# A graph network layer: the turning of h moved from TensorE to DMA, ahead of its use

## The chip, the cores and the metric

The kernel runs on one core of a Trainium2 chip. The metric is device time in microseconds (us) of one launch. PE is TensorE (PEld its weight loads), DVE is VectorE, ACT is ScalarE, POOL is GpSimd, SP is SyncE, which here only issues DMAs.

## What is computed

64 graphs of 256 nodes with 256 channels, float32. After a layer norm without weights and a ReLU, `h` goes through one network layer:

```python
h = jnp.maximum(_layernorm(x, axis=-1), 0.0)
x = x + _L0_gnn_ref(h, adj, ...)
# inside, with x = h:
xc = jnp.transpose(x, (0, 2, 1))
h = relu(_bn(_conv1d(xc, conv1_w, 0), bn1...))        # 1 tap
h = _bn(_conv1d(h, conv2_w, 8), bn2...)               # 17 taps
x_conv = jnp.transpose(relu(h + xc), (0, 2, 1))
s = x @ w_se.T + b_se
A = jnp.exp(-dist(s)) * mask                          # mask is adj
msg = relu(x @ w_msg.T + b_msg)
x_nmp = jnp.einsum('bnm,bmd->bnd', A, msg)
gi = concat([x_conv, x_nmp]) @ w_ih.T + b_ih
gh = x @ w_hh.T + b_hh
r, z = sigmoid(gi_r + gh_r), sigmoid(gi_z + gh_z)
return (1 - z) * tanh(gi_n + r * gh_n) + z * x
```

## The kernel before, in words

**Tiling.** A block `i` is two graphs (W = 512 nodes); there are 32 blocks. Four blocks make a batch `b` of eight graphs; the eight batches run one after the other. In the loop `i = 4b` is the batch's first block and `nxt = i + 4` the first of the next batch, so that block numbers such as `nxt + 2` mean work done ahead.

**From x to hT.** `load_x` brings a block of rows to `x` (two buffers), with nodes on partitions. `norm_steps` (L507) makes the statistics on DVE (L518 to L523), the power -0.5 on POOL (L524) and scales `x` in place on DVE (L527). `transpose_h` (L590) turns the block on PE: eight 128x128 transposes against the identity (helper at L484) into `aux` banks of PSUM, and two ReLUs on ACT (L600) write `hT`, with channels on partitions. Then it issues the load of block `i + 2`. `hT` feeds `conv1`, `message`, `gates` and `residual`.

**The convolution of 17 taps** is done for a batch at a time in a transformed domain. `conv1` (w_c1 on PE, ReLU on ACT to `h`) and `split_steps` (DVE, writes U and V) prepare each block of the next batch; `forward` puts the odd and even forward transforms (DVE) in the planner's queue; `products` (eight calls a batch) multiplies by weights `wb`, streamed from DRAM by SP with nine buffers; `branch_back`, `q_back`, `p_back` and `join` go back on DVE, and `residual` (L719, then ReLU L720 on ACT) leaves x_conv in `Yv`. V and Yu are one memory.

**The rest of a block.** `message` makes msg and s; `embed` and `affinity` make exp(-dist) (L760, L761) and multiply by `ADJ` on DVE (L767); `aggregate` makes `xnm`; `gates` (L794) is called twice a block, once for each half of the output channels, and does 36 matmul passes of 128x512: the terms of h and xnm first, those of `Yv` last, with a hook `early` after the first third and `wait` ahead of the terms of `Yv`. `finish` turns the result back on PE (8 transposes), adds it to `Y` and stores it.

**adj.** Its columns are wanted in the order of `Yv`. From block 3 on `turn_adj` turns a block by a DMA transpose (512 KB, as pairs of uint16 halves) into the tile `halves` (one buffer), `keep_adj` writes it to DRAM in four DMAs of 1 KB rows (L403), `load_adj` (POOL queue) brings it back, and `join_adj` puts the halves together in two copies on ACT (L423). Before the change it is called at the end of `aggregate`.

**What sets the order.** Each engine runs its instructions in the order of the program, which is written out by hand. DVE work without a fixed place goes through `pace` (L234): a queue of steps that are put between the fixed DVE instructions where a running estimate of PE's and DVE's time leaves room; `pace.flush(mark)` empties it up to a mark. SP and POOL issue their DMAs in order too, and an issue that waits holds all behind it.

Of the kernel before, what the change touches and what calls it, by code (L numbers as in the profile page):

```python
# [301 lines left out]
def kernel(  # L302
# [122 lines left out]
    def load_y(i):  # L425
        Y[i] = late.tile([P, G * MC, D], FP, name="y", bufs=2)
        load_rows(Y[i], x, i, nc.gpsimd)
# [78 lines left out]

    def norm_steps(i):  # L507
# [5 lines left out]
        def stats(j):  # L513
            if j == 0:
                t["st"] = work.tile([P, G * MC, 6], FP, name="st")
                t["mv"] = work.tile([P, G * MC, 2], FP, name="mv")
                t["rstd"] = work.tile([P, G * MC], FP, name="rstd")
            nc.vector.bn_stats(t["st"][:, j, :], X[i][:, j, :])  # L518

        def aggregate_stats():  # L520
# [3 lines left out]
            nc.gpsimd.tensor_tensor(t["rstd"], t["rstd"], neg_half, ALU.pow)  # L524

# [63 lines left out]
    def transpose_h(i):  # L589
# [11 lines left out]
        if i + 2 < B // G:  # L601
            load_x(i + 2, nc.gpsimd if i < 2 else nc.sync)

# [178 lines left out]
    def aggregate(i):  # L782
# [8 lines left out]
        join_adj(i + 1)  # L791
# [49 lines left out]
    def finish(i):  # L841
# [8 lines left out]
        if i + 2 < B // G:  # L850
            load_y(i + 2)
# [11 lines left out]
    odd, even, normed, halved = (Mark() for _ in range(4))  # L863
# [53 lines left out]
    for b in range(NB):  # L917
# [17 lines left out]
        pace.flush(even)  # L935
        pace.add(fft.branch_back(Yv, T, 2))
        pace.add(fft.odd_back(Yv, T))
        aggregate(i)
        if b == 0:
# [6 lines left out]
        norm(nxt)  # L946
        affinity(i + 1)
        if b > 0:
            load_adj(i + 2)
        products(b, 6)  # L950
        if b == 0:
            transpose_a(i + 1)
        transpose_h(nxt)
        products(b, 7)
        pace.add(mix(fft.p_back(Yu, T), fft.q_factors(Yu)))
# [4 lines left out]
        stats, scale = norm_steps(nxt + 1)  # L960
        join(0)
        pace.add(stats)
        join(1)
        pace.add(scale, normed)
        pace.add(split_steps(nxt), halved)
        join(2)
        join(3)
# [109 lines left out]
```

## Time and profile before

| | |
|---|---|
| median of 12 runs (lowest to highest) | 1891.92 us (1886.38 to 1898.74) |
| the profiled execution's own time | 1889.53 us |
| its span, first to last instruction | 1887.5 us |
| mean granted clock of TensorE | 0.993 |
| DMA moved | 217.63 MB, mean 115 GB/s |
| `message(i + 2)` of batch 2 starts at | 617.38 us |
| `message(i + 2)` of batch 3 starts at | 839.01 us |

The first batch's inputs and the weights' transforms fill the first 120 us or so; a batch in the middle takes 839.01 - 617.38 = 221.6 us. Such a batch has a stage of `products` (about 57 us), in which SP streams `wb`, and a long stage of `gates` (about 165 us), in which the next batch is prepared. A row of a timeline gives start, duration, engine, line, operation, output and inputs, count, and in brackets the idle time of the engine before it with what ended it. A PE row's duration runs over into the next, so durations are taken here from start to start.

### The profile page before, as it was taken

What the parts mean: (1) busy time and instruction counts of PE and PEld (TensorE: products, weight loads), DVE (VectorE), ACT (ScalarE), POOL (GpSimd) and SP (SyncE); (2) the same over time, 40 slices, a digit from 0 to 9 for tenths busy, and PEclk for the clock granted to TensorE, in tenths of its full rate; (3) what the DMA queues carried; (4) which work ended last, traced back from release to release, by engine and by line L of the source; (5) the groups of instructions that cost most, each with busy time, mean ns of one, the idle gap of its engine ahead of it and who ended that gap; (6) DMA issues with size and microseconds to landing.
All of it is one profiled execution on the core that took longest, in us unless ns stands there. A gap on an engine that the chain in (4) does not pass through costs nothing.

```text
span 1887.5 us, 21985 instructions
## 1 busy us (share of the span) xinstructions
PE 1831.2 (97%) x7710; PEld 1137.2 (60%) x7710; DVE 1398.0 (74%) x2675; ACT 637.4 (34%) x1335; POOL 215.3 (11%) x340
## 2 busy tenths in 40 slices
PE   6999999999999999999999999999999999999997
PEld 3686454865459554784458655495546944587443
DVE  5878548996499946998389964999459983798522
ACT  2524332254222532244222443134432352224321
POOL 3210111010111010111101101110101111010000
PEclk9999999999999999999999999999999999999999
DMA  6886431761328341482316623284314823063010
GB/s 186 266 277 154 89 79 45 214 160 56 81 62 246 88 107 38 133 220 63 82 41 198 170 58 86 47 243 108 91 55 109 243 56 78 23 183 108 1 45 23
DMA packets 178526, 217.63 MB, mean 115 GB/s; under 512 B 85378, under 2 KB 105118, under 8 KB 178417
## 3 DMA queue, kind: packets, MB, share of 16 engines
q1 hardware_dynamic: 144373, 153.87, 28.9%
q0 software_dynamic: 31936, 60.48, 12.9%
q10 hardware_dynamic: 2108, 1.89, 0.3%
q8 instruction: 61, 1.00, 0.2%
q14 instruction: 48, 0.39, 0.1%
HBM read 156.54 MB, written 44.30 MB: 106 GB/s over the span
## 4 chain that ended last, share of the span: by engine, by line
PE 82%; DVE 8%; DMA 3%; issue 3%; ACT 2%; POOL 1%; POOLq 0%; ACTq 0%; DVEq 0%
PE acc L480 70%; PE aux L480 8%; PE aux L484 3%; DVE Yv L59 1%; PE aux L760 1%; DVE e L767 1%; DVE Yv L62 1%; DMA points<-points 1%; DVE T L65 1%; DVE Yv L65 1%; DMA x<-in_x_dram 1%; DMA wb<-filt 1%; POOL filt L648 1%; DVE msg L732 1%; DVE V L65 1%
## 5 line engine op out<-in xcount | busy, mean ns | idle before, releaser
L480 PE MATMUL acc<-hT,w_hh 128*128 128x512 f32 x768 | 354.6, 598 | 3.6 <-ACT h L619 3.6
L480 PE MATMUL acc<-xnm,w_ih 128*128 128x512 f32 x768 | 353.7, 595 | 0.0
L480 PE MATMUL acc<-Yv,w_ih 128*128 128x512 f32 x768 | 341.1, 593 | 9.6 <-ACT Yv L720 9.6
L480 PEld LDWEIGHTS acc<-Yv,w_ih 128*128 128x128 f32 x768 | 145.2, 190 | 196.5 <-issue 177.3
L480 PEld LDWEIGHTS acc<-xnm,w_ih 128*128 128x128 f32 x768 | 145.8, 191 | 183.6 <-issue 181.6
L480 PEld LDWEIGHTS acc<-hT,w_hh 128*128 128x128 f32 x768 | 143.8, 192 | 171.6 <-issue 161.9
L821 ACT ACTIVATE tr<-acc,b_rz 128x512 f32<-128x512 f32 x64 | 44.0, 687 | 542.0 <-PE acc L480 542.0
L823 DVE SCALAR_TENSOR_TENSOR gn<-tr,gn 128x512 f32<-128x512 f32 x64 | 44.2, 691 | 210.2 <-ACT tr L821 210.2
L849 POOL DMA_DIRECT2D out_dram<-y x64 | 39.0, 615 | 890.7 <-DVE y L848 860.9
L480 PE MATMUL acc<-U,wb 128*128 128x128 f32 x1024 | 124.8, 276 | 1.0 <-DMA wb<-filt 1.0
L480 PE MATMUL acc<-V,wb 128*128 128x128 f32 x1024 | 124.8, 275 | 0.0
L480 PEld LDWEIGHTS acc<-U,wb 128*128 128x128 f32 x1024 | 120.5, 192 | 4.9 <-DVE Yv L59 2.3
L59 DVE SCALAR_TENSOR_TENSOR V<-T,V 128x256 f32<-128x256 f32 (+2 forms) x224 | 121.6, 612 | 0.3
L480 PE MATMUL acc<-hT,w_c 128*128 128x512 f32 x256 | 117.8, 604 | 1.9 <-ACT hT L600 1.0
L480 PEld LDWEIGHTS acc<-V,wb 128*128 128x128 f32 x1024 | 119.5, 192 | 0.0
L480 PE MATMUL aux<-e,msg 128*128 128x256 f32 x464 | 104.9, 379 | 0.0
L480 PEld LDWEIGHTS aux<-e,msg 128*128 128x128 f32 x464 | 86.1, 190 | 11.4 <-issue 1.0
L848 DVE TENSOR_TENSOR y<-aux,y 128x512 f32<-128x512 f32 x64 | 41.1, 684 | 68.4 <-PE aux L484 68.4
L524 POOL TENSOR_TENSOR rstd<-rstd,neg_half 128x4 f32<-128x4 f32 x32 | 36.3, 1134 | 470.9 <-DVE rstd L523 470.8
L480 PE MATMUL aux<-w_msg,hT 128*128 128x259 f32 x384 | 89.4, 382 | 0.0
L527 DVE TENSOR_SCALAR x<-x,mv,rstd 128x256 f32<-128x256 f32 x128 | 44.3, 409 | 52.1 <-POOL rstd L524 52.1
L480 PEld LDWEIGHTS acc<-hT,w_c 128*128 128x128 f32 x256 | 49.2, 194 | 51.9 <-issue 45.6
(149 smaller groups left out, 2741.8 us busy)
## 6 DMA issues: line engine op xcount, KB each, us to landing
wb<-filt SPq DMA_DIRECT2D x376, 256.0 KB
y<-in_x_dram POOLq DMA_DIRECT2D x64, 256.0 KB, 5.4
out_dram<-y POOLq DMA_DIRECT2D x64, 256.0 KB, 5.2
x<-in_x_dram SPq DMA_DIRECT2D x60, 256.0 KB
halves_d<-halves SPq DMA_DIRECT2D x116, 128.0 KB
adjh<-halves_d POOLq DMA_DIRECT2D x116, 128.0 KB, 5.3
filt<-fo POOLq DMA_DIRECT2D x20, 252.0 KB, 5.4
filt<-fo SPq DMA_DIRECT2D x16, 252.0 KB
```

Source lines behind the costliest of these rows:

```text
L59: return self.step(out, lambda: self.v.scalar_tensor_tensor(out, x, s, y, op0=ALU.mult, op1=ALU.add))
L62: return self.step(out, lambda: self.v.tensor_add(out, x, y))
L65: return self.step(out, lambda: self.v.tensor_sub(out, x, y))
L480: nc.tensor.matmul(p, w, v, **kw)
L484: nc.tensor.transpose(p, v, ident)
L524: nc.gpsimd.tensor_tensor(t["rstd"], t["rstd"], neg_half, ALU.pow)
L527: nc.vector.tensor_scalar(X[i][:, j, :], X[i][:, j, :], t["mv"][:, j, 0:1], t["rstd"][:, j:j + 1], ALU.subtract, ALU.mult)
L648: eng.dma_start(out=filt[m][g * KG:g * KG + size].rearrange("k t c o -> (k t) (c o)"), in_=t[:size * kinds])
L821: nc.scalar.activation(tr, pr, AF.Tanh, bias=b_rz[:, dc:dc + 1], scale=0.5)
L823: nc.vector.scalar_tensor_tensor(gn, tr, 1.0, gn, op0=ALU.add, op1=ALU.mult)
L848: nc.vector.tensor_add(row_tile(Y[i], g), p, row_tile(Y[i], g))
L849: nc.gpsimd.dma_start(out=rows(out, G * i + g), in_=row_tile(Y[i], g))
```

## The change

The first five blocks still go the old way. From block 5 on (blocks 5 to 31, 27 in all) h is made thus:

- No scaling of `x` on DVE. Two small operations (DVE, POOL) make `shift` beside `rstd`.
- `turn_h`: four activations on ACT write relu(x * rstd + shift) into the tile `hh`, in blocks of 64 channels; a DMA transpose on SP (`hh` to `halves`, 512 KB from SBUF to SBUF); then the load of `x`.
- `sort_h`: four DMAs on SP in rows of 1 KB bring `halves` to a second `hh` (the same buffer).
- `join_h`: two copies on ACT put the halves together in `hT`.

`halves` has one buffer, shared by the turnings of h and of adj, and `hh` one, shared by the source of the turning and the sorted rows. The calls stand one ahead of the other: in a batch `turn_h(nxt + 1)` stands behind `message(i + 2)`, `join_h(nxt + 1)` in the second `gates`, `turn_h(nxt + 2)` right behind it, and so on; `turn_h(nxt + 4)` stands in the fifth `gates` and is joined in the next batch's `products`, where that block is `nxt`.

Moved are: `conv1(nxt)` from ahead of the first `gates` into its `wait`; `embed` and `affinity` into the hooks of `gates`; `conv1(nxt + 1)` ahead of `aggregate(i + 2)`; `join_adj` out of `aggregate`; the statistics of `nxt + 1` into `products`; `forward` ahead of `gates(i + 2, 0)`; the last two `join`s later. `Y` has one buffer in place of two.

What this does to the order on three engines is shown in the third batch (b = 2). **PE**, from the end of the first `gates` on (`Yv,w_ih` are the last terms of a call of `gates`, `ident,x` is a turning of h, `e,msg` is `aggregate`, `w_c` is `conv1`). Before:

```order
L480 MATMUL acc<-Yv,w_ih 128x512 x6
L480 MATMUL acc<-hT,w_hh 128x512 x4
L480 MATMUL acc<-xnm,w_ih 128x512 x4
L480 MATMUL acc<-hT,w_hh 128x512 x2
L480 MATMUL acc<-xnm,w_ih 128x512 x2
L480 MATMUL acc<-Yv,w_ih 128x512 x6
L484 MATMUL aux<-ident,x 128x128 x8
L480 MATMUL aux<-e,msg 128x256 x8
L480 MATMUL acc<-hT,w_c_95 128x512 x4
```

and now:

```order
L480 MATMUL acc<-hT,w_c_95 128x512 x4
L480 MATMUL acc<-Yv,w_ih 128x512 x6
L480 MATMUL acc<-hT,w_hh 128x512 x4
L480 MATMUL acc<-xnm,w_ih 128x512 x4
L480 MATMUL acc<-hT,w_hh 128x512 x2
L480 MATMUL acc<-xnm,w_ih 128x512 x2
L480 MATMUL acc<-Yv,w_ih 128x512 x6
L480 MATMUL acc<-hT,w_c_95 128x512 x4
L480 MATMUL aux<-e,msg 128x256 x8
```

The eight transposes are gone, `conv1` of the next block follows `gates` at once, and the earlier `conv1` stands inside the first `gates`.

**ACT**, in the second `gates` and behind it (`gn`, `tr`, `nn`, `tz` belong to `gates`, `h` to `conv1`, `adj` to `join_adj`). Before:

```order
L810 ACTIVATE gn<-acc,bn_columns 128x512
L821 ACTIVATE tr<-acc,b_rz 128x512
L720 ACTIVATE Yv<-Yv,bn_shift 128x512 x4
L828 ACTIVATE nn<-gn,bn_columns 128x512
L831 ACTIVATE tz<-acc,b_rz 128x512
L720 ACTIVATE Yv<-Yv,bn_shift 128x512
L600 ACTIVATE hT<-aux 128x512 x2
L790 ACTIVATE xnm<-aux 128x512 x2
L423 COPY adj<-adjh 128x2x2x256 x2
L619 ACTIVATE h_143<-acc,bn_shift,bn_scale 128x2x16x16 x2
```

and now:

```order
L852 ACTIVATE gn<-acc,bn_columns 128x512
L645 COPY hT<-hh 128x1024 x2
L622 ACTIVATE hh<-x,shift,rstd 128x4x64 x4
L863 ACTIVATE tr<-acc,b_rz 128x512
L763 ACTIVATE Yv<-Yv,bn_shift 128x512 x2
L870 ACTIVATE nn<-gn,bn_columns 128x512
L873 ACTIVATE tz<-acc,b_rz 128x512
L662 ACTIVATE h_144<-acc,bn_shift,bn_scale 128x2x16x16 x2
L833 ACTIVATE xnm<-aux 128x512 x2
L423 COPY adj<-adjh 128x2x2x256 x2
```

The joining copies and the scalings for the next turning stand between `gn` and `tr` of one call of `gates`, and `conv1`'s ReLUs now stand ahead of the copies of adj.

**SP**, behind the last `wb` of `products`. Before (the load of `x` is block `nxt + 2`):

```order
L659 DMA wb<-filt_145 128x512 x6
L394 DMA_TRANSPOSE halves<-in_adj_dram 128x4x512
L403 DMA halves_d<-halves 4x32x512 x4
L394 DMA_TRANSPOSE halves<-in_adj_dram 128x4x512
L377 DMA x<-in_x_dram 128x1x512 x2
```

and now:

```order
L702 DMA wb<-filt_146 128x512 x9
L625 DMA_TRANSPOSE halves<-hh 128x16x128
L377 DMA x<-in_x_dram 128x1x512 x2
L636 DMA hh<-halves 64x2x512 x4
L394 DMA_TRANSPOSE halves<-in_adj_dram 128x4x512
L403 DMA halves_d<-halves 4x32x512 x4
L625 DMA_TRANSPOSE halves<-hh 128x16x128
```

A turning of h with its four sorting DMAs stands ahead of each turning of adj with its four; no load of `x` is left among the `wb`.

```diff
-        Y[i] = late.tile([P, G * MC, D], FP, name="y", bufs=2)
+        Y[i] = late.tile([P, G * MC, D], FP, name="y")
...
+            if i > PB:
+                nc.vector.tensor_scalar(t["shift"], t["mv"][:, :, 0], -1.0, None, ALU.mult)
+                nc.gpsimd.tensor_tensor(t["shift"], t["shift"], t["rstd"], ALU.mult)
...
+    TURNED, HH = {}, {}
+    HP = P // 2
+    def turn_h(i):
+        if i >= B // G:
+            return
+        t = late.tile([P, 2 * MC, W], U16, name="hh").bitcast(FP)
+        h = t.rearrange("p k (q d) -> p k q d", d=HP)
+        for q in range(G * MC):
+            nc.scalar.activation(h[:, :, q], X[i][:, q, :].rearrange("p (k d) -> p k d", d=HP), AF.Relu,
+                                 scale=STATS[i]["rstd"][:, q:q + 1], bias=STATS[i]["shift"][:, q:q + 1])
+        TURNED[i] = late.tile([P, 2 * MC, W], U16, name="halves")
+        nc.sync.dma_start_transpose(out=TURNED[i].rearrange("p k (q n) -> p (k q) n", n=P),
+                                    in_=t.rearrange("p k d -> p (k d)").bitcast(U16))
+        if i + 2 < B // G:
+            load_x(i + 2)
+    def sort_h(i):
+        if i >= B // G:
+            return
+        HH[i] = late.tile([P, 2 * MC, W], U16, name="hh")
+        for j in range(2):
+            for k in range(2):
+                nc.sync.dma_start(out=HH[i][k * HP:(k + 1) * HP, j::2, :], in_=TURNED[i][j::2, k::2, :])
+    def join_h(i):
+        if i >= B // G:
+            return
+        HT[i] = work.tile([P, DC, W], FP, name="hT", bufs=6)
+        v = HT[i].bitcast(U16).rearrange("p c (n j) -> p j c n", j=2)
+        u = HH[i].rearrange("p (c j) n -> p j c n", j=2)
+        for j in range(2):
+            nc.scalar.copy(v[:, j], u[:, j])
...
-        if i + 2 < B // G:
-            load_y(i + 2)
+        if i + 1 < B // G:
+            load_y(i + 1)
...
+        if b == 0:
+            norm(nxt)
+        else:
+            run(norm_steps(nxt + 1)[0])
         pace.add(fft.branch_back(Yv, T, 2))
         pace.add(fft.odd_back(Yv, T))
         aggregate(i)
-        if b == 0:
+        if b > 0:
+            join_adj(i + 1)
+        else:
             nc.gpsimd.dma_start(out=w_hh, in_=hh_wT.rearrange("(k p) o -> p k o", p=P))
             nc.gpsimd.dma_start(out=w_ih, in_=ih_wT.rearrange("(k p) o -> p k o", p=P))
         products(b, 4)
         message(i + 1)
         products(b, 5, lambda i=i: embed(i + 1))
         pace.add(mix(fft.q_back(Yu, T), fft.odd_factors(Yv)))
-        norm(nxt)
+        if b == 0:
+            pace.add(norm_steps(nxt + 1)[0], normed[1])
         affinity(i + 1)
         if b > 0:
             load_adj(i + 2)
+            join_h(nxt)
         products(b, 6)
         if b == 0:
             transpose_a(i + 1)
-        transpose_h(nxt)
+            transpose_h(nxt)
         products(b, 7)
-        pace.add(mix(fft.p_back(Yu, T), fft.q_factors(Yu)))
+        pace.add(mix(fft.p_back(Yu, T), fft.q_factors(Yu)), scaled)
         def join(j):
             pace.add(fft.join(Yu, Yv, T, slice(2 * G * j, 2 * G * (j + 1))))
             pace.add([(W, lambda o=o: residual(i + j, o)) for o in range(DC)], joined[j])
-        stats, scale = norm_steps(nxt + 1)
         join(0)
-        pace.add(stats)
+        pace.add(norm_steps(nxt + 2)[0], normed[2])
         join(1)
-        pace.add(scale, normed)
-        pace.add(split_steps(nxt), halved)
-        join(2)
-        join(3)
         if b == 0:
             turn_adj(3)
             keep_adj(3)
         aggregate(i + 1)
+        if b > 0:
+            join_adj(i + 2)
         message(i + 2)
-        conv1(nxt)
-        embed(i + 2)
-
-        def wait(j=0):
-            pace.flush(joined[j])
-        gates(i, 0, wait, lambda i=i: affinity(i + 2, True))
+        pace.flush(normed[1])
+        turn_h(nxt + 1)
+
+        def wait():
+            pace.flush(scaled)
+            affinity(i + 2, True)
+            conv1(nxt)
+            pace.add(split_steps(nxt), halved)
+            join(2)
+            pace.flush(joined[0])
+        gates(i, 0, wait, lambda i=i: embed(i + 2))
         if b == 0:
             transpose_a(i + 2)
+            load_y(0)
         load_adj(i + 3)
+        sort_h(nxt + 1)
         turn_adj(nxt)
-        if b == 0:
-            load_y(0)
-            load_y(1)
-        gates(i, 1)
         keep_adj(nxt)
-        turn_adj(nxt + 1)
-        pace.flush(normed)
-        transpose_h(nxt + 1)
-        aggregate(i + 2)
+
+        def early():
+            join_h(nxt + 1)
+            pace.flush(normed[2])
+            turn_h(nxt + 2)
+        gates(i, 1, None, early)
         pace.flush(halved)
         conv1(nxt + 1)
-        stats, scale = norm_steps(nxt + 2)
-        pace.add(stats)
+        join(3)
         pace.add(split_steps(nxt + 1), halved)
-        pace.add(scale, normed)
+        pace.add(norm_steps(nxt + 3)[0], normed[3])
+        aggregate(i + 2)
+        join_adj(i + 3)
         pace.flush(joined[1])
-        gates(i + 1, 0)
+        sort_h(nxt + 2)
+        turn_adj(nxt + 1)
         keep_adj(nxt + 1)
+        gates(i + 1, 0, lambda nxt=nxt: join_h(nxt + 2))
+        pace.flush(normed[3])
+        turn_h(nxt + 3)
+        pace.flush(halved)
+        conv1(nxt + 2)
+        pace.add(split_steps(nxt + 2), halved)
+        pace.add(norm_steps(nxt + 4)[0], normed[0])
+        finish(i)
+        sort_h(nxt + 3)
         turn_adj(nxt + 2)
-        pace.flush(normed)
-        transpose_h(nxt + 2)
+        keep_adj(nxt + 2)
+        gates(i + 1, 1)
+        join_h(nxt + 3)
         message(i + 3)
-        conv1(nxt + 2)
-        stats, scale = norm_steps(nxt + 3)
-        pace.add(stats)
-        pace.add(split_steps(nxt + 2), halved)
-        pace.add(scale, normed)
-        finish(i)
-        embed(i + 3)
-        gates(i + 1, 1)
-        keep_adj(nxt + 2)
-        turn_adj(nxt + 3)
-        affinity(i + 3)
-        load_adj(nxt)
-        gates(i + 2, 0)
-        keep_adj(nxt + 3)
-        pace.flush(normed)
-        transpose_h(nxt + 3)
-        aggregate(i + 3)
         conv1(nxt + 3)
         pace.add(split_steps(nxt + 3), halved)
         if b + 1 < NB:
             forward()
+        pace.flush(normed[0])
+        pace.flush(joined[2])
+
+        def wait():
+            affinity(i + 3)
+            turn_h(nxt + 4)
+        gates(i + 2, 0, wait, lambda i=i: embed(i + 3))
+        sort_h(nxt + 4)
+        turn_adj(nxt + 3)
+        keep_adj(nxt + 3)
+        aggregate(i + 3)
         finish(i + 1)
+        load_adj(nxt)
         gates(i + 2, 1)
+        join_adj(nxt)
+        pace.flush(joined[3])
         gates(i + 3, 0)
         finish(i + 2)
         gates(i + 3, 1)
```

More of the change, by code (lines that the diff above doesn't have):

```diff
@@ L504, in columns @@
         return [c[:, sum(n[:j]):sum(n[:j + 1])] for j in range(len(n))]
+    STATS = {}
     def norm_steps(i):
@@ L515, in stats @@
                 t["st"] = work.tile([P, G * MC, 6], FP, name="st")
-                t["mv"] = work.tile([P, G * MC, 2], FP, name="mv")
-                t["rstd"] = work.tile([P, G * MC], FP, name="rstd")
+                t["mv"] = work.tile([P, G * MC, 2], FP, name="mv", bufs=2)
+                t["rstd"] = work.tile([P, G * MC], FP, name="rstd", bufs=2)
+                t["shift"] = work.tile([P, G * MC], FP, name="shift", bufs=2)
+                STATS[i] = t
             nc.vector.bn_stats(t["st"][:, j, :], X[i][:, j, :])
@@ L790, in aggregate @@
             nc.scalar.activation(XNM[i][:, dc, :], p, AF.Copy)
-        join_adj(i + 1)
     OT = {}
@@ L861, in mix @@
         return q
-    odd, even, normed, halved = (Mark() for _ in range(4))
+    odd, even, halved, scaled = (Mark() for _ in range(4))
+    normed = [Mark() for _ in range(PB)]
     joined = [Mark() for _ in range(PB)]
```

## The prediction

> **What bounds the kernel.** I read the page's engine shares and its chain first, then the stages of one batch.
>
> ```profile
> PE 1831.2 (97%) x7710; PEld 1137.2 (60%) x7710; DVE 1398.0 (74%) x2675; ACT 637.4 (34%) x1335; POOL 215.3 (11%) x340
> PE 82%; DVE 8%; DMA 3%; issue 3%; ACT 2%; POOL 1%; POOLq 0%; ACTq 0%; DVEq 0%
> ```
>
> ```profile
> core 0: us, PE busy (x) PEld busy (x) DVE busy (x) ACT busy (x) POOL busy (x), PEclk, DMA share, GB/s
> 617.38:782.20 164.82, 163.30 (x472) 82.18 (x470) 119.42 (x217) 58.28 (x109) 17.82 (x27) 1.00 0.29 72
> 782.20:839.01 56.81, 56.75 (x464) 54.28 (x462) 54.26 (x116) 18.00 (x51) 5.89 (x9) 1.00 0.80 237
> ```
>
> PE is busy for 97% and carries 82% of the chain. In the gates stage of batch 2 (first row) it is busy 163.30 of 164.82 us while DVE, ACT and the DMA engines have room; in the products stage DVE (54.26 of 56.81) and DMA (0.80) are nearly as full as PE. So what PE does less of comes off the time, as long as nothing that PE needs arrives late. The timeline of PE gives the pieces:
>
> ```profile
> 635.22 1.88 PE L480 MATMUL acc<-xnm,w_ih 128*128 128x512 f32 x4
> 638.16 5.42 PE L480 MATMUL acc<-Yv,w_ih 128*128 128x512 f32 x12 [1.06 <-ACT Yv L720]
> 643.41 3.60 PE L480 MATMUL acc<-hT,w_hh 128*128 128x512 f32 x8
> ...
> 658.86 1.04 PE L484 MATMUL aux<-ident,x 128*128 128x128 f32 x8
> 659.74 3.62 PE L480 MATMUL aux<-e,msg 128*128 128x256 f32 x16
> 663.19 3.60 PE L480 MATMUL acc<-hT,w_c 128*128 128x512 f32 x8
> 666.62 3.60 PE L480 MATMUL acc<-hT,w_hh 128*128 128x512 f32 x8
> ...
> 682.95 2.79 PE L480 MATMUL aux<-w_msg,hT 128*128 128x259 f32 x12
> ...
> 686.45 3.60 PE L480 MATMUL acc<-hT,w_c 128*128 128x512 f32 x8
> ```
>
> From start to start a turning of h is 659.74 - 658.86 = 0.88 us, `aggregate` 3.45, `conv1` 3.43 (0.43 a pass), `message` 3.50, a call of `gates` 658.86 - 643.41 = 15.45, two thirds of it ahead of the terms of `Yv`.
>
> **Term 1: the transposes.** 27 blocks lose eight transposes each: 27 x 0.88 = 23.8 us of PE. They overlap nothing else of PE, so all of it is on the path.
>
> **Term 2: the wait for Yv.** At 635.22 four passes start (1.72 us); the next should follow at 636.94 and starts at 638.16, so 1.22 us are lost, 1.06 of them idle. The list of waits has eight of these, one a batch:
>
> ```profile
> PE acc L480 <- ACT Yv L720: 9.6, 8, 1.8
> ```
>
> Six like this one, in batches 1 to 6, are 7.3 us; the other 9.6 - 6 x 1.06 = 3.2, in the first and the last batch, I leave in. The change leaves PE as much work ahead of it (`conv1` only moves inside the `gates`), so it goes only if DVE gets there sooner. What stands ahead of the residual on DVE:
>
> ```profile
> 852.66 2.13 DVE L767 TENSOR_TENSOR e<-e,adj 128x256 f32<-128x256 f32 x4 [0.31 <-ACT e L761]
> ...
> 858.16 1.41 DVE L719 SCALAR_TENSOR_TENSOR Yv<-Yv,bn_scale,hT 128x512 f32<-128x512 f32 x2
> ```
>
> In the new order the four products with adj (854.68 - 852.66 = 2.02 us and a wait of 0.31) come behind this residual, the four scalings of `x` (409 ns each, row L527 below) are gone, and the forward transforms end ahead of `products`. 2.3 us alone covers the 1.22. I take the term whole: 7.3 us.
>
> **Term 3: two long waits, in the first and the last batch.** PE and then ACT in batch 0:
>
> ```profile
> 220.08 3.60 PE L480 MATMUL acc<-xnm,w_ih 128*128 128x512 f32 x8
> 227.27 3.78 PE L480 MATMUL acc<-hT,w_hh 128*128 128x512 f32 x4 [3.60 <-ACT h L619]
> 230.85 3.00 PE L480 MATMUL acc<-xnm,w_ih 128*128 128x512 f32 x4
> 233.68 2.74 PE L480 MATMUL acc<-Yv,w_ih 128*128 128x512 f32 x6
> ```
>
> ```profile
> 224.07 2.51 ACT L423 COPY adj<-adjh 128x1024 uint16<-128x1024 uint16 x2 [10.06 <-DMA adjh<-halves_d]
> ```
>
> ACT waited 10.06 us for adj of block 3, and `conv1`'s ReLU, on which PE's bank hung, stood behind. PE should have gone on at 220.08 + 3.44 = 223.52, lost 3.75 us, and then ran slowly: eight passes from 227.27 to 233.68 took 6.41 us in place of 3.44. Together 6.7 us. Now that ReLU stands ahead of the copies; behind them come a whole `gates` of PE work (15.45) before `conv1(6)` needs the ACT queue's `hT`. I count 6.7. In the last batch:
>
> ```profile
> 1727.24 1.04 PE L480 MATMUL acc<-w_msg,hT 128*128 128x259 f32 x4
> 1731.20 1.25 PE L484 MATMUL aux<-ident,z 128*128 128x128 f32 x3 [2.92 <-ACT z L736]
> 1732.24 4.95 PE L480 MATMUL acc<-hT,w_hh 128*128 128x512 f32 x8
> 1737.03 1.88 PE L480 MATMUL acc<-xnm,w_ih 128*128 128x512 f32 x4
> ```
>
> `embed` waited there for z from 1728.1 to 1731.20 (3.1), and the eight passes took 4.79 for 3.44: 4.4 us with both. Now a third of `gates` (5.15 us) stands ahead of `embed`. I count 4.4.
>
> **What is added.** ACT, from the page's groups and the listing by line:
>
> ```profile
> L423 ACT COPY adj<-adjh 128x1024 uint16<-128x1024 uint16 x58 | 73.6, 1339 | 10.1 <-DMA adjh<-halves_d 10.1
> L761 ACT ACTIVATE e<-aux 128x256 f32<-128x256 f32 x104 | 32.9, 385 | 47.6 <-PE acc L760 28.4 <-PE aux L760 19.2
> L600 ACT ACTIVATE hT<-aux 128x512 f32<-128x512 f32 x62 | 33.4, 593 | 8.7 <-PE aux L484 8.7
> L527 DVE TENSOR_SCALAR x<-x,mv,rstd 128x256 f32<-128x256 f32 x128 | 44.3, 409 | 52.1 <-POOL rstd L524 52.1
> ```
>
> Two joining copies, taken as those of adj (same shape), 2.68 us, and four scalings of 128x256, taken as row L761, 1.54, replace two ReLUs (1.19): 3.0 us more a block, 12 a batch, beside 164.82 - 58.28 = 106 us of idle ACT in the gates stage. They count only where ACT holds PE up. In the second `gates` they stand between `gn` and `tr`: 4.2 us, while PE still has 24 of its 36 passes (10.3 us) to do before `tr` has its sum; hidden, and 4.2 a call if PE had nothing left there. One place is tight: `join_h(nxt + 3)` stands behind the last activation of a `gates`, and its buffer is free only after a DVE operation behind that: about 0.7 + 0.7 + 2.5 = 3.9 us, and PE has only `message` (3.50) ahead of `conv1(nxt + 3)`. I add 0.4 us a batch, seven times (b = 0 to 6): 2.8 us. On DVE the scalings' 1.6 us a block go and one small operation comes; POOL's extra multiply stands about a call of `gates` ahead of its use; the loads of `x` leave the stream of `wb`, in whose stage the DMA share is 0.80. I put these at nothing, since DVE and DMA lose work there. `Y` with one buffer makes POOL wait behind each store, with two calls of `gates` (30.9 us) to the next use and one (15.45) at the very end; were that too short, the last `finish` would wait for one load.
>
> **The one chain that decides: SP.** `halves` is one buffer, so turning h, sorting it, turning adj and writing it out follow one another. A turning from SBUF and a sort are not in this trace; the nearest rows are the turning of adj, of the same 512 KB, and its four DMAs, once with the streams quiet and once behind the last `wb`:
>
> ```profile
> 1557.64 2.33 SPq L394 DMA_TRANSPOSE halves<-in_adj_dram  x1
> 1561.98 2.23 SPq L403 DMA_DIRECT2D halves_d<-halves  x4
> 1569.76 2.01 SPq L394 DMA_TRANSPOSE halves<-in_adj_dram  x1
> ```
>
> ```profile
> 838.61 5.59 SPq L394 DMA_TRANSPOSE halves<-in_adj_dram  x1
> 847.77 2.38 SPq L403 DMA_DIRECT2D halves_d<-halves  x4
> 855.57 1.89 SPq L394 DMA_TRANSPOSE halves<-in_adj_dram  x1
> ```
>
> Each next row starts when the one before has landed. So turning and four row DMAs, H, take 4.34 + 7.78 = 12.1 us quiet and 9.16 + 7.80 = 17.0 crowded; below, the issues alone are 2.01 + 2.23 = 4.2. The gates stage has no `wb` (share 0.29), so I take the quiet 12.1 for h as for adj. Now the deadlines, counted from the last product. PE does `aggregate`, `message`, `gates`, `conv1`, `gates`: `conv1(nxt + 1)` comes at 41.3 us; `conv1(nxt + 2)` after 3.43 + 3.45 + 15.45 more, 63.6; `conv1(nxt + 3)` after 3.43 + 0.88 + 15.45 + 3.50 more, 86.9. Less 2.5 for the copies the sorted rows must be there by 38.8, 61.1 and 84.4. The first scaling ends at about 13 (message's PE end at 7, its own ACT work, 1.5; an estimate). The rows land at 13 + H, 13 + 3H, 13 + 5H: 25, 49 and 74; the third can't start before its scaling behind the third `gates`, about 66, so 78. All in time, the tightest by 6 us, and H may grow to 14.3. Cost in the forecast: nothing.
>
> [...]
>
> **Sum.** 1889.5 (the profiled execution) - 23.8 - 7.3 - 6.7 - 4.4 + 2.8 = 1850.1. That execution lies 2.4 below the median of the 12 runs, so 1852.5; I say 1852.
>
> **Rivals.**
>
> A. *New waits for old.* ACT and DVE get in the way after all, in two or three places a batch: the wait for `Yv` stays, `conv1` waits for `hT`, and those of the first and last batch turn up elsewhere. For it: DVE is at 54.26 of 56.81 in the products stage, so that a step placed a little wrong there shows at once. Against it: DVE loses work there. Then only term 1 is left: 1889.5 - 23.8 + 2.4 = 1868. Chance 0.20.
>
> B. *The loop over `halves` is longer than PE's (slower).* From H = 14.3 on the third block's rows come after their `conv1`; five H's pile up, and PE's wait brings slow passes behind it, as in batch 0 (6.41 for 3.44, 3 us). The savings, 42.2 us, are 6.0 for each of seven batches: 3 us late and 3 of slow passes, so it turns to a loss at 13 + 5H = 87.4, H = 14.9. With the crowded row's 17.0 the third rows land at 98, 13.4 late: 16.4 a batch, 1889.5 - 42.2 + 115 + 2.4 = 1965. For it: the load of `x` and POOL's stores now run between these DMAs, and H lies just 2.2 under the point. Against it: the sorting DMAs stay in SBUF, and the crowded row had the last `wb` beside it. Chance 0.13.
>
> C. *A turning out of SBUF is several times as slow as one out of DRAM.* [...] Chance 0.03, since the two turnings quoted take 4.34 and 9.16. [...]
>
> D. *Nothing to gain*, because another engine takes over all of term 1: 0.02, near 1890. Only the products stage is near such a bound, and just 0.88 of a batch's 3.5 us of transposes lie in it.
>
> **How the numbers follow.** Forecast 0.62, A 0.20, B 0.13, C 0.03, D 0.02. 0.2% of the time (3.8 us) is about what a measurement of this kernel can tell from no change. The forecast alone reaches from 1840 (the 2.8 not arising, the 3.2 of the other two `Yv` waits gone, and some smaller ones) to 1860. With A, which may be up to 14 us dearer than its middle, the range is 1840 to 1882, 0.82 of the chance; the lower bound of H changes nothing, the upper one is B, left out. Faster: forecast, A and the mild end of B, 0.83; same 0.03; slower: most of B, and C, 0.14.
>
> **What would show it.** PE: the group `aux<-ident,x` at 40 instructions in place of 256; no wait for `Yv` L763 in the middle batches; the 3.60 and 2.92 us waits gone; a batch in the middle shorter by 3.5 + 1.2 - 0.4 = 4.3 us. SP: `hh` turning and sort in about 12 us. Wrong would be the forecast if PE waits for ACT's `hT` L645, and ACT for `hh<-halves`, with clock below 1.00 behind it; the waits name B or C by the length of the `DMA_TRANSPOSE` to its sort. If instead ACT or DVE are named without a DMA behind them, it is A.

## The result and the profile after

| | before | after |
|---|---|---|
| median (lowest to highest) | 1891.5 us (1886.38 to 1898.74), 32 runs | 1845.41 us (1841.74 to 1849.17), 8 runs |
| the profiled execution, its span | 1889.53, 1887.5 us | 1843.07, 1841.3 us |

The ratio is 0.9753, 95% interval 0.9741 to 0.9766: 2.5% faster. Forecast were 1852 us and a range of 1840 to 1882.

First the page of the changed kernel, its busy times and its chain:

```profile
PE 1801.3 (98%) x7494; PEld 1114.8 (61%) x7494; DVE 1366.7 (74%) x2594; ACT 729.7 (40%) x1443; POOL 225.4 (12%) x367
PE 91%; DMA 4%; DVE 2%; issue 1%; ACT 1%; POOL 1%; POOLq 0%; SPq 0%; ACTq 0%; DVEq 0%
```

PE has 216 instructions less (27 blocks of 8 transposes) and 29.9 us less busy time; ACT has 92 us more, and still the chain is more PE's than before (91% against 82%). Next the windows of the stages of batch 2, gates and products, cut at `message(i + 2)` as before:

```profile
core 0: us, PE busy (x) PEld busy (x) DVE busy (x) ACT busy (x) POOL busy (x), PEclk, DMA share, GB/s
601.00:761.91 160.91, 160.45 (x447) 79.67 (x446) 123.61 (x228) 70.54 (x125) 18.81 (x30) 1.00 0.41 95
761.91:817.78 55.87, 55.83 (x456) 53.41 (x455) 45.45 (x93) 19.37 (x51) 6.46 (x10) 1.00 0.84 252
```

The gates stage went from 164.82 to 160.91 us, the products stage from 56.81 to 55.87. In the gates stage PE was idle for 1.52 us and is now for 0.46. DVE is no longer near its limit in the products stage (45.45 of 55.87, before 54.26 of 56.81). The groups of the listing by line that the prediction named:

```profile
L484 PE MATMUL aux<-ident,x 128*128 128x128 f32 x40 | 6.5, 308 | 3.0 <-DVE x L534 3.0
L480 PE MATMUL acc<-Yv,w_ih 128*128 128x512 f32 x768 | 341.0, 593 | 1.1 <-ACT Yv L763 1.1
L645 ACT COPY hT<-hh 128x1024 uint16<-128x1024 uint16 x54 | 69.0, 1351 | 1.3 <-DMA hh<-halves 1.3
L622 ACT ACTIVATE hh<-x,shift,rstd 128x256 f32<-128x256 f32 x108 | 55.9, 593 | 2.2 <-POOL shift L531 1.6
```

40 transposes of `x` are left. One wait for `Yv` is left, 1.1 us in the last batch. ACT waited 1.3 us in all for sorted rows. The scalings take 593 ns in this group and not the 385 of the row that I had taken for them; four in a row fill about 2.1 us of ACT (849.59 to 851.66 in batch 3) where the prediction had 1.54. Here is PE around the place of the old wait, one batch of the changed kernel:

```profile
613.42 1.88 PE L480 MATMUL acc<-xnm,w_ih 128*128 128x512 f32 x4
615.23 0.71 PE L803 MATMUL aux<-zT 9*128 9x256 f32 x6
616.40 0.69 PE L803 MATMUL aux<-zT 9*128 9x256 f32 x2 [0.46 <-ACT e L804]
617.02 3.70 PE L480 MATMUL acc<-hT,w_c 128*128 128x512 f32 x8
620.56 4.88 PE L480 MATMUL acc<-Yv,w_ih 128*128 128x512 f32 x11
```

The passes with `Yv` follow `conv1` (617.02) without a wait. What is left in a batch is the pause at 616.40, which stood in the kernel before too: `affinity` has four tiles and `aux` three banks, so the fourth waits for ACT (e7 below tests this).

The one place at which I had added time is `conv1(nxt + 3)` behind the copies of `join_h(nxt + 3)`. ACT in one batch, and PE in the first batch and in that one:

```profile
900.29 0.69 ACT L873 ACTIVATE tz<-acc,b_rz 128x512 f32<-128x512 f32 x1 [0.33 <-PE acc L480]
900.88 2.54 ACT L645 COPY hT<-hh 128x1024 uint16<-128x1024 uint16 x2
```

```profile
253.12 3.70 PE L480 MATMUL acc<-hT,w_c 128*128 128x512 f32 x8 [0.85 <-ACT hT L645]
...
903.54 3.63 PE L480 MATMUL acc<-hT,w_c 128*128 128x512 f32 x8
```

The copies follow `tz` at once and end at 903.42; `conv1` starts at 903.54, without a wait. Only the first batch has one, and its cause is another, as the copies there show:

```profile
250.53 2.53 ACT L645 COPY hT<-hh 128x1024 uint16<-128x1024 uint16 x2 [0.99 <-DMA hh<-halves]
```

ACT was ready there and waited for the sorted rows. SP's chain was late: its first turning was issued 14.4 us after the start of `message(i + 2)` (179.83 less 165.47; in batch 3 it is 10.3), and two of its turnings with their sorts took 16.8 and 17.0 us (179.83 to 196.59 and 234.27 to 251.28).

Where the 46.2 us of span went is seen best by batches. The times here are taken from the starts of PE's instructions in each trace: the first product of the first batch, then from the first product of one batch to that of the next, and in the last batch to the start of PE's last instruction.

| us | first product | first batch | batches 1 to 6, each | last batch |
|---|---|---|---|---|
| before | 104.9 | 234.0 | 221.6 | 210.7 |
| after | 108.1 | 220.2 | 216.8 | 204.0 |
| e1, h on PE | 105.8 | 221.8 | 220.7 | 205.7 |
| e2, turned twice | 107.2 | 234.2 | 222.2 to 228.1, the sixth 216.8 | 205.4 |
| e3, turned thrice | 112.0 | 245.7 | 231.5 to 235.5 | 205.7 |
| e4, new kernel, old piece | 107.2 | 219.7 | 218.6 to 221.5 | 208.4 |
| e5, old kernel, copies later | 107.9 | 227.2 | 221.6 | 210.6 |
| e6, old kernel, new piece | 105.8 | 231.5 | 226.4 to 227.6 | 206.7 |
| e7, more banks | 112.0 | 218.0 | 215.6 | 205.3 |
| e8, as e6, ACT otherwise | 107.6 | 235.0 | 228.5 to 228.7 | 213.0 |
| e9, as e6, ACT otherwise | 109.3 | 230.8 | 221.6 | 206.4 |
| e10, e9 with join(3) later | 109.9 | 231.3 | 220.3 | 206.4 |
| e11, scalings on DVE too | 113.7 | 219.8 | 216.9 | 204.0 |

So 13.8 us come from the first batch, 6 x 4.83 = 29.0 from the middle, 6.7 from the last, and 3.2 are lost ahead of the first product. That start lies between 104.9 and 113.7 in these traces, and the change adds, moves or removes no instruction of PE, DVE, ACT or POOL in the first 100 us; the cause of the spread stays open.

### The profile page after: what moved, and what is told of

Read it like the earlier page. It is cut to its first block, busy times and chain, and to the rows that moved or that the text cites. A ratio compares the mean times of both kernels' runs of the same rounds, so it can differ in the third digit from the quotient of the medians.

```text
span 1841.3 us, 21875 instructions
## 1 busy us (share of the span) xinstructions
PE 1801.3 (98%) x7494; PEld 1114.8 (61%) x7494; DVE 1366.7 (74%) x2594; ACT 729.7 (40%) x1443; POOL 225.4 (12%) x367
## 3 DMA queue, kind: packets, MB, share of 16 engines
q0 software_dynamic: 31936, 60.48, 14.3%
## 4 chain that ended last, share of the span: by engine, by line
PE 91%; DMA 4%; DVE 2%; issue 1%; ACT 1%; POOL 1%; POOLq 0%; SPq 0%; ACTq 0%; DVEq 0%
PE acc L480 77%; PE aux L480 9%; PE aux L484 2%; PE aux L803 1%; DMA filt<-fo 1%; DMA points<-points 1%; DMA x<-in_x_dram 1%; DVE Yv L59 0%; DMA halves<-hh 0%; DMA hh<-halves 0%; POOL filt L691 0%; DVE Yv L62 0%; DVE T L65 0%; DMA b_msg<-in_msg_b_dram 0%; DVE msg L775 0%
## 5 line engine op out<-in xcount | busy, mean ns | idle before, releaser
L480 PE MATMUL acc<-hT,w_hh 128*128 128x512 f32 x768 | 350.5, 592 | 0.0
L891 POOL DMA_DIRECT2D out_dram<-y x64 | 39.4, 620 | 795.3 <-DVE y L890 794.0
L480 PE MATMUL aux<-e,msg 128*128 128x256 f32 x464 | 104.9, 379 | 0.0
L870 ACT ACTIVATE nn<-gn,bn_columns 128x512 f32<-128x512 f32 x64 | 46.2, 722 | 115.7 <-DVE gn L868 115.7
L423 ACT COPY adj<-adjh 128x1024 uint16<-128x1024 uint16 x58 | 73.9, 1344 | 23.0 <-DMA adjh<-halves_d 23.0
```

The source lines that it names most:

```text
L423: nc.scalar.copy(v[:, j], u[:, j])
L480: nc.tensor.matmul(p, w, v, **kw)
L870: nc.scalar.activation(nn, gn, AF.Tanh, bias=b_ih[:, 2 * DC + dc:2 * DC + dc + 1])
L891: nc.gpsimd.dma_start(out=rows(out, G * i + g), in_=row_tile(Y[i], g))
```

## Experiments

The theory: PE bounds the kernel, so transposes off PE are worth their PE time, and the moved pieces take away three kinds of waits. Rivals: the new order or a lighter DVE carries the whole gain; the loop of turnings over `halves` is near its limit. A half loop is a turning and the four DMAs behind it, H in the prediction. In the diffs `...` and shortened arguments stand for what is left out.

**e1: h turned by PE at the new places.** `turn_h` only scales, `sort_h` does nothing:

```diff
 def join_h(i):
-    for j in range(2):
-        nc.scalar.copy(v[:, j], u[:, j])
+    for dc in range(DC):
+        p = aux()
+        for j in range(G * MC):
+            transpose(chunk(p, j // MC, j % MC), HH[i][:, j, dc * P:(dc + 1) * P])
+        nc.scalar.copy(HT[i][:, dc, :], p)
```

> The changed kernel, with h turned by PE again: the block is still normalized by ACT at the new places, but no DMA turns or sorts it; at each place of join_h eight transposes of 128x128 and two copies of 128x512 out of PSUM stand. If PE is what bounds the kernel, the 27 blocks cost 27 x 0.88 = 23.8 us again and nothing else comes back: 1845.4 + 23.8 = 1869 us (1865 to 1873). The rival, that most of the gain is the new order and DVE's lighter load: under 1855. The other rival, that the loop of turnings and sorts was holding something up that this takes away: also under 1869, and then waits for hh or hT are to be seen in the changed kernel at the places where they are gone here.

Measured: 1871.33 us (ratio to before 0.9900, 0.9871 to 0.9930), 25.9 above the changed kernel. A middle batch is 3.95 us longer: 4 x 0.88 = 3.52, and a new pause of 0.45 us for a bank of `aux` ahead of one group of transposes:

```profile
591.26 1.09 PE L484 MATMUL aux<-ident,hh 128*128 128x128 f32 x8 [0.45 <-ACT e L796]
```

Inside the batches its profile is 26.8 us longer than that of the changed kernel. The transposes make about 23.8 of it and six such pauses 2.7, and the 0.85 us wait of the first batch is gone. The last batch, which turns nothing, is 1.7 longer: a wait of 1.08 us for `Yv` stands there in both kernels, but in e1 the twelve passes behind it ran slowly (a row of 7.11 us and not 5.42). So term 1 is shown at its price. The other 20 us of the gain are there without any turning by DMA.

**e2 and e3: each turning of h issued two and three times.**

```diff
-        nc.sync.dma_start_transpose(out=..., in_=...)
+        for _ in range(2):
+            nc.sync.dma_start_transpose(out=..., in_=...)
```

> The changed kernel, with each turning of h issued twice into the same tile (the second repeats the first). A half loop of h grows by the 4.3 us of a turning. By the deadlines of the prediction (rows of the third block at 13 + 3 x 16.4 + 2 x 12.1 = 86.4 against 84.4) the third block comes 2 us late in each of seven batches: 14 us, 1859. By the trace of the changed kernel the third rows land 4.4 us ahead of their copies, and the chain behind a second turning is slack by some of its 8.6: 1.5 us a batch, 1856 (1846 to 1870). If the loop has room to spare: 1845 to 1847.

> The same with each turning of h issued three times: half loops of h longer by 8.7 us. By the rival with the long loop, the third block's conv1 waits about 13 + 3 x 20.8 + 2 x 12.1 - 84.4 = 15.2 us in each of seven batches, and slow passes of 3 us follow each long wait: 7 x 18 = 127, some 1970 us (1920 to 2000), slower than the kernel before. If PE's wait for it is hidden, under 1880.

Measured: e2 1893.3 us (ratio 1.0008, 0.9992 to 1.0024), e3 1972.91 (1.0427, 1.0403 to 1.0450). One more turning a block, 4.3 to 4.4 us in batch 3 of the changed kernel, eats up the whole gain; the 1859 and 1856 expected of e2 were far off. The time of e3 came out as forecast, but by other waits: fourteen for `hT`, two a batch and 93.9 us in all, the longest 12.1, where one of 15.2 a batch was expected. That the sums agree is luck. The lists of waits, first of e2, then of e3:

```profile
PE acc L480 <- ACT hT L646: 41.7, 7, 12.1
PE acc L480 <- ACT hT L646: 93.9, 14, 12.1
```

SP's queue shows why. First the changed kernel, then e2, in batch 3 (the loads of `x` left out):

```profile
828.12 1.78 SPq L625 DMA_TRANSPOSE halves<-hh  x1
832.50 2.66 SPq L636 DMA_DIRECT2D hh<-halves  x4
839.16 1.99 SPq L394 DMA_TRANSPOSE halves<-in_adj_dram  x1
844.30 2.33 SPq L403 DMA_DIRECT2D halves_d<-halves  x4
852.69 1.71 SPq L625 DMA_TRANSPOSE halves<-hh  x1
857.05 3.53 SPq L636 DMA_DIRECT2D hh<-halves  x4
863.26 1.97 SPq L394 DMA_TRANSPOSE halves<-in_adj_dram  x1
...
883.21 1.71 SPq L625 DMA_TRANSPOSE halves<-hh  x1
887.47 4.70 SPq L636 DMA_DIRECT2D hh<-halves  x4
896.51 3.00 SPq L394 DMA_TRANSPOSE halves<-in_adj_dram  x1
```

```profile
853.55 6.29 SPq L626 DMA_TRANSPOSE halves<-hh  x2
...
883.53 6.09 SPq L626 DMA_TRANSPOSE halves<-hh  x2
892.03 2.65 SPq L637 DMA_DIRECT2D hh<-halves  x4
898.50 1.92 SPq L394 DMA_TRANSPOSE halves<-in_adj_dram  x1
902.76 2.33 SPq L403 DMA_DIRECT2D halves_d<-halves  x4
911.35 12.12 SPq L626 DMA_TRANSPOSE halves<-hh  x2
925.61 2.99 SPq L637 DMA_DIRECT2D hh<-halves  x4
931.56 2.50 SPq L394 DMA_TRANSPOSE halves<-in_adj_dram  x1
```

In the changed kernel a turning out of SBUF takes 4.3 to 4.4 us to the next step (828.12 to 832.50, 852.69 to 857.05, 883.21 to 887.47), beside 4.34 for one out of DRAM in the kernel before (1557.64 to 1561.98). The longest of all, in the first batch, took 8.1 (234.27 to 242.35, DMA share 0.84). Half loops of h take 11.0, 10.6 and 13.3 us, the first of adj 13.5. The third rows are there by 896.51, and their copies start at 900.88: 4.4 us to spare. In e2 the third turning starts when the DMAs ahead of it have left `halves`, and the pair takes 14.3 us (911.35 to 925.61) where the pair at 883.53 took 8.5. Meanwhile POOL stores `y` and loads the next (its issues stand at 910.76 and 917.69 us), and the DMA share is 0.92, beside 0.70 for the other pair; that this traffic is the cause is argued, not shown. Those rows land at 931, and PE waits:

```profile
930.98 2.51 ACT L646 COPY hT<-hh 128x1024 uint16<-128x1024 uint16 x2 [4.57 <-DMA hh<-halves]
```

```profile
933.55 5.39 PE L480 MATMUL acc<-hT,w_c 128*128 128x512 f32 x8 [4.42 <-ACT hT L646]
```

The eight passes behind the wait start over 5.23 us in place of 3.44. So rival B is the right mechanism, and its point fits: it had the rows late from H = 14.3 on and the gain eaten up at 14.9. Here the five half loops take 78.0 us (853.55 to 931.56), 15.6 on average, and the time is that of before; in batch 6 they take 71.4 (1532.83 to 1604.27), 14.3 on average, and PE doesn't wait. The change lies less than one turning a block away from that point.

**e4: the new kernel with the old piece around the first gates**, that is `conv1(nxt)` and `embed` ahead of them, and `affinity` with its products with adj ahead of the residual.

```diff
         message(i + 2)
+        conv1(nxt)
+        embed(i + 2)
         pace.flush(normed[1])
         turn_h(nxt + 1)
+        pace.add(split_steps(nxt), halved)
+        join(2)
...
-        gates(i, 0, wait, lambda i=i: embed(i + 2))
+        def early():
+            pace.flush(scaled)
+            affinity(i + 2, True)      # its products placed at once, not by pace
+        gates(i, 0, lambda: pace.flush(joined[0]), early)
```

> The changed kernel with the piece around the first gates of a batch as before: conv1(nxt) and embed(i + 2) ahead of gates, affinity in the place of embed, and the four products with adj ahead of the residual of joined[0] on DVE. The forward transforms and the scalings stay as changed. If the order of DVE is what removed the wait for Yv, it comes back with about 1.3 us in 8 batches, and z in the last batch makes embed wait again (up to 3.1 us): 1845.4 + 10 to 14 = 1855 to 1860. If the missing scalings or the earlier forward transforms removed it, the wait stays away, and the time is within 4 us of 1845.

Measured: 1862.19 us (ratio 0.9840, 0.9823 to 0.9857), 16.8 above the changed kernel, but the wait has another name:

```profile
836.75 0.71 PE L803 MATMUL aux<-zT 9*128 9x256 f32 x6
838.98 0.69 PE L803 MATMUL aux<-zT 9*128 9x256 f32 x2 [1.51 <-ACT e L804]
```

ACT's new scalings (834.96 to 837.04) and two of the inverse transforms (L68) stand ahead of the exponentials (838.55), so `affinity` loses 1.05 us more than the 0.46 it always lost. With PE that much later `Yv` is nearly in time (1.2 us in five waits). The last batch waits 2.9 us for z again. The place is worth what was forecast and more; whose order it is, this run doesn't tell. Hence e6 to e10, which change the kernel before.

**e5: the kernel before, copies of adj of block 3 behind conv1(5).**

```diff
-        join_adj(i + 1)            # end of aggregate(i)
+        if i != 2:
+            join_adj(i + 1)
...
         conv1(nxt + 1)
+        if b == 0:
+            join_adj(3)
```

> The kernel before with one thing moved in batch 0: the joining copies of adj of block 3 stand behind the ReLU of conv1(5) in place of ahead of it. By the prediction PE's wait of 3.60 us in front of that gates goes, and the slow passes behind it (6.41 us for 3.44): 6.7 us less, 1884.8. The rival: the DMA that the copies wait for holds up the next thing on ACT instead, hT of block 6 or affinity of block 3: 0 to 3 us less.

Measured: the wait is gone and the first batch is 234.03 - 227.20 = 6.83 us shorter (6.7 forecast); the other batches are unchanged. The median, 1888.16 us, is only 3.0 below before (ratio 0.9980, 0.9968 to 0.9991); in the profile the first product starts 3.0 later, which the edit doesn't explain.

**e6, e8, e9: the kernel before with the new piece around the first gates.** PE runs the same instructions in the same order in all three, and so does DVE in e8 and e9; in e6 a few DVE instructions a batch (`gn` and scalings of `x`) stand some places apart. What differs is ACT's order.

```diff
-        conv1(nxt)
-        embed(i + 2)
-        gates(i, 0, lambda: pace.flush(joined[0]), lambda: affinity(i + 2, True))
+        def wait():
+            pace.flush(scaled)                                    # e9 alone
+            affinity(i + 2, True, lambda: pace.flush(joined[0]))  # between exponentials and products; e6: ahead of both
+            conv1(nxt)
+        gates(i, 0, wait, lambda: embed(i + 2))
```

> The kernel before with the piece around the first gates of a batch in the new order: embed(i + 2) in early, then in wait the residual of joined[0] on DVE, then affinity(i + 2) with its four products, and conv1(nxt). The four scalings and the forward transforms stay as before. If the order alone carries these two terms, the waits for Yv of batches 1 to 6 go (7.3) and embed's wait for z in the last batch with the slow passes (4.4): 11.7 less, 1879.8. If DVE's lighter load is needed for the first, only 4.4 less: 1887.

> The kernel before with the piece around the first gates of a batch in the new order on all engines: embed(i + 2) in early; in wait the tiles and exponentials of affinity(i + 2), then the residual of joined[0] with its ReLU, then the four products with adj, then conv1(nxt). In e6 the ReLU of the residual stood ahead of the exponentials on ACT, and affinity waited 4.4 us; here it stands behind. The four scalings and the forward transforms stay as before. If the order alone carries the wait for Yv and the one for z, both go: 7.3 + 4.4 = 11.7 less than before, and up to 3.2 more if the waits of the first and the last batch go too: 1880 (1876 to 1882). If DVE's lighter load is needed, only z's 4.4 goes: 1887.

> As e8, with one thing more: the eight scalings of the inverse transforms on ACT (L68, 4.3 us) stand ahead of the exponentials of affinity, not behind. In e8 they stood behind, DVE waited 6.62 us for them, and PE 5.24 for Yv. PE and DVE have the same rows in the same order in e6, e8 and this kernel; only ACT's order differs: scalings, ReLU, exponentials in e6 (1919 us), exponentials, scalings, ReLU in e8 (1936), scalings, exponentials, ReLU here, as in the changed kernel. If that order carries the two terms: 1880 (1876 to 1882), with no wait for Yv in batches 1 to 6 and none for z. If DVE's lighter load is needed for the wait for Yv: 1887. If there is one more thing that e6 and e8 lacked: over 1892.

Measured: e6 1919.18 us (ratio 1.0147, 1.0128 to 1.0166), e8 1936.08 (1.0236, 1.0222 to 1.0250), e9 1886.41 (0.9964, 0.9950 to 0.9978). Rows of ACT and PE in e6:

```profile
638.43 1.33 ACT L720 ACTIVATE Yv<-Yv,bn_shift 128x512 f32<-128x512 f32 x2 [3.85 <-DVE Yv L719]
639.67 0.91 ACT L761 ACTIVATE e<-aux 128x256 f32<-128x256 f32 x3
```

```profile
640.09 1.11 PE L760 MATMUL aux<-zT 9*128 9x256 f32 x2 [4.40 <-ACT e L761]
```

The ReLU waits for DVE, the exponentials stand behind it, and PE waits for their bank. In e8 the exponentials come first, but ahead of the scalings (L68) on which DVE's joins depend, and this is DVE and then PE:

```profile
648.54 0.69 DVE L62 TENSOR_TENSOR T<-V 128x512 f32<-128x512 f32 x1 [6.62 <-ACT V L68]
```

```profile
652.82 8.21 PE L480 MATMUL acc<-Yv,w_ih 128*128 128x512 f32 x12 [5.24 <-ACT Yv L720]
```

In e9 both are right, and `Yv` is in time in batches 1 to 6. Yet a batch takes 221.61 us as before, for 24 us later PE shows this:

```profile
659.50 1.89 PE L480 MATMUL aux<-e,msg 128*128 128x256 f32 x8
662.46 1.99 PE L480 MATMUL aux<-e,msg 128*128 128x256 f32 x8 [1.06 <-ACT hT L600]
```

1.23 us (662.46 - 659.50 less 1.73 for eight passes): the old loss in a new place. Only the last batch (210.7 to 206.4) and the first (234.0 to 230.8) gained. In the last the wait for z is gone and the terms of `Yv` start 6.0 us earlier in the batch, but the passes behind the 1.08 us wait for `Yv` that is left there ran slowly, as in e1, and took 1.5 us of it back.

**e10: e9 with join(3) behind conv1(nxt + 1).**

```diff
         join(2)
-        join(3)
...
         conv1(nxt + 1)
+        join(3)
```

> As e9, with join(3) (two joins and two residuals, 4.2 us of DVE) put behind conv1(nxt + 1), as in the changed kernel. In e9 the wait for Yv was gone, but 1.22 us came back 24 us later in each of batches 1 to 6, where aggregate waits for a bank of aux until ACT's hT has left it; ahead of that, DVE worked without a break for 20 us and ACT stood behind it. If DVE's backlog there is the cause, the second wait goes too: 6 x 1.22 = 7.3 less than e9, 1879 (1877 to 1881). If it is the bank of aux and the transposes of h that use it, nothing changes: 1886.

Measured: 1877.51 us (ratio 0.9926, 0.9907 to 0.9945), a middle batch 1.3 shorter, and `aggregate` runs through:

```profile
658.49 1.04 PE L484 MATMUL aux<-ident,x 128*128 128x128 f32 x8
659.36 3.62 PE L480 MATMUL aux<-e,msg 128*128 128x256 f32 x16
```

DVE's backlog it was, not the bank: its 4.2 us of `join(3)` held back the operations on which ACT's queue, and with it hT, hung.

**e11: the new kernel, DVE scaling x once more** into a tile that nobody reads.

```diff
         for q in range(G * MC):
+            nc.vector.tensor_scalar(u, X[i][:, q, :], mv, rstd, ALU.subtract, ALU.mult)
             nc.scalar.activation(h[:, :, q], ...)
```

> The changed kernel, with DVE scaling each block of x once more into a tile that nobody reads (4 x 409 ns, as before the change) ahead of ACT's scalings. If the four scalings taken off DVE are part of the gain, up to 1.2 us in each of seven batches come back: 1854. If the new order leaves DVE room for them (it sits idle for 2.23 us ahead of the first joins): 1845 to 1847.

Measured: 1846.13 us (ratio 0.9757, 0.9736 to 0.9778), a middle batch 0.1 longer. In the new order the scalings on DVE cost next to nothing.

**e7: a bank more for affinity.**

```diff
-            affinity(i + 2, True)
-            conv1(nxt)
+            affinity(i + 2)        # fourth tile in acc
+            conv1(nxt, True)       # conv1: p = aux() if spare and o else acc()
```

> The changed kernel, where the fourth tile of affinity(i + 2) in the first call of gates takes a bank of acc in place of a fourth of aux (which has three), and the second output of conv1(nxt) takes one of aux. PE then no longer waits for ACT's e between the third and the fourth tile: 0.46 us idle and 0.8 from start to start, in 8 batches: 6.4 us less, 1839 (1837 to 1842). If the wait for Yv, 1.4 us later, takes its place: 1845.

Measured: 1838.82 us (ratio 0.9717, 0.9700 to 0.9735), 6.6 below the changed kernel and the fastest here. In the same place as above the four tiles of `affinity`, two passes each, now follow at once:

```profile
615.72 0.49 PE L803 MATMUL aux<-zT 9*128 9x256 f32 x3
615.74 0.48 PE L803 MATMUL acc<-zT 9*128 9x256 f32 x1
616.04 0.39 PE L803 MATMUL aux<-zT 9*128 9x256 f32 x3
616.06 0.37 PE L803 MATMUL acc<-zT 9*128 9x256 f32 x1
616.37 1.98 PE L480 MATMUL acc<-hT,w_c 128*128 128x512 f32 x4
```

A middle batch is 1.15 us shorter: the eight passes take 0.65 us (615.72 to 616.37) in place of 1.79 (615.23 to 617.02). The last batch is 1.3 us longer than in the changed kernel: with no `conv1` as cover the wait for `Yv` grew from 1.08 to 1.88 us, which left 0.35 of the saving, and the twelve passes behind it ran slowly again (7.11 for 5.42).

## Why the prediction was right, step by step

- **Term 1** (23.8): right. The 216 transposes are gone, and putting them back (e1) costs 25.9, with six new pauses and slow passes in the last batch among it.
- **Term 2** (7.3): right in size, its reason incomplete. The wait went in batches 1 to 6. I put it down to four products with adj behind the residual on DVE, with the scalings and the earlier forward transforms as a margin. e9 has the first without the other two: the wait goes, and 1.23 us come back at `aggregate`. The step that lacked was what stands later in the same queue: `join(3)` also had to move (e10, -1.3 a batch). The scalings have no part in it (e11), and the forward transforms were as before in e10. ACT's order, which the prediction didn't look at here, decides more than either: 1936 or 1886 us with PE and DVE in the same order (e8, e9), 1919 with all but a few DVE instructions in it (e6). The changed kernel has that order of ACT and `join(3)` later too, and so the term came true whole; the prediction gave no reason for either, and so far that was luck.
- **Term 3** (6.7 and 4.4): right. e5 gives 6.8 in the first batch. In the last the wait for z is gone in e9; that its last batch is shorter by 4.3, so near the term, is luck, the sum of 6.0 gained by the terms of `Yv` and slow passes behind them.
- **Added 2.8**: mis-sized. It arose nowhere: the copies of `join_h(nxt + 3)` (900.88 to 903.42) just end ahead of `conv1` (903.54). The 3.9 us had a wait for a buffer in it that didn't come. The one wait at this place, 0.85 us in the first batch, is SP's.
- **The 3.2 left in**: 2.1 of it went. In the first batch the short waits of PE for `e` and `wb` went too, which I hadn't counted: `message(i + 2)` starts 57.4 us behind the first product (108.10 to 165.47) and not 61.0 (104.92 to 165.92), 3.6 less. These and the 2.8 are most of the 10.1 us by which the gain inside the batches (49.5) exceeds the forecast (1889.5 - 1850.1 = 39.4); 3.2 of the gain are lost ahead of the batches.
- **SP's chain at no cost**: right in batches 1 to 6, where the third rows come 4.2 us or more ahead of their copies; I had 6. In the first batch they came 1.0 us late and cost PE 0.85. H for h came out at 9.6 to 13.5 us in batches 1 to 6 and up to 17.0 in the first, and at 13.3 to 13.9, not 12.1, for the first turning of adj in batches 1 to 6. In e2's forecast the steps that failed were to take a turning at its quiet 4.3 us wherever it stands, and to leave out the slow passes behind a wait and the first batch, where one wait is 12.1 us.
- **The whole.** The old kernel with e10's order takes 1877.5 us; less term 1 (23.8) and e5's 6.8 this makes an estimate of 1846.9, and the changed kernel takes 1845.4. So the parts tested here account for the gain, within 1.5 us.
- **Rivals.** A (1868) fell: the waits were gone, and no new one for ACT or DVE came in their place. B is real and was avoided by less than one turning a block; the 0.85 us in the first batch, with PE waiting for `hT` and ACT for `hh<-halves`, is the sign that the prediction had named for it. C fell, a case for which the trace of before had no row: turnings out of SBUF take 4.26 to 4.38 us in batch 3 of the changed kernel and 8.1 at the longest, in the first batch, beside 4.34 and 9.16 out of DRAM in the kernel before.

## What to carry to other kernels

Take a wait away only together with a look at what stands behind it in the same engine's queue: e9 removed one entirely, and the time of a batch didn't change until DVE's next backlog was moved too. Where one engine serves two others, write down its order first: ACT's three orders spread the same work over 50 us (1886.41 us in e9 to 1936.08 in e8). And price a DMA chain at what it takes in its place, with its slack beside it: here a pair of turnings took 8.5 us in one place and 14.3 in another, and one more turning a block, 4.3 us in the changed kernel, cost 48 (e2).

## What the runs showed of the hardware

In these runs slow passes of PE follow a wait of the same length in one batch and not in another. In e4 PE sits idle for 1.49 to 1.51 us at the same place in six batches; in three of them passes of 128x512 behind it take up to 0.9 us in place of 0.43. In the last batch of the changed kernel, e1 and e9 a wait of 1.08 us stands at the same place, and the passes behind it are slow in e1 and e9 alone. The windows of two places of e4, a slow one and a quick one:

```profile
617.98:621.50 3.52, 3.52 (x6) 1.41 (x5) 3.48 (x7) 0.41 (x2) 0.00 (x0) 0.50 0.78 181
1277.65:1281.20 3.55, 3.55 (x10) 1.57 (x9) 3.52 (x7) 0.55 (x2) 0.00 (x0) 1.00 0.81 174
```

The granted clock is 0.50 in one and 1.00 in the other. In batch 3, one of the slow ones, the 1.51 us of idle time stand among the eight short passes of `affinity` (836.75 to 839.60), and the four passes of 128x512 behind them start over 3.48 us (839.60 to 843.08) in place of 1.72. Why the passes are slow in one batch and not in another, no run here shows.
